# Expert weights of a mixture-of-experts block held in separated pieces of 2 KB and 1 KB

## Chip, cores and metric

The kernel runs on one core of one Trainium2 chip. The metric is the device time of one execution in microseconds; lower is better. The core's engines are TensorE (PE in the profile, with PEld for its weight loads), VectorE (DVE), ScalarE (ACT), GpSimd (POOL) and SyncE (SP); transfers run on 16 DMA engines, which SP and GpSimd feed from a queue each.

## The reference

One block of a perceiver-like network on 64 sequences of 32 tokens with 256 features (2048 tokens), float32 throughout. Three residual steps follow one another: cross-attention with 16 heads to a context of 257 rows for each sequence, self-attention with 4 heads within a sequence, and a mixture of 8 experts of which each token uses 2. The last one is what the change concerns:

```python
x = x + xattn(layernorm(x), ctx_512, ...)
x = x + attn(layernorm(x), ...)
x = x + ffn(layernorm(x), ...)

# ffn
scores = x @ Wr.T + br
w = softmax(scores); idx = top_k(scores + biases_N, 2)
val = w[idx] / sum(w[idx])
h = x @ Wl1[n] + bl1[n]                 # [M, 2*512] for each expert n
a, b = h[..., :512], h[..., 512:]
y[n] = (silu(a) * b) @ Wl2[n] + bl2[n]  # [M, 256]
out = sum over the token's two experts of val * y[n]
```

## The kernel before

**Tokens and experts.** The 2048 tokens are taken as 16 tiles of 128. The attention steps of neighbouring tiles are interleaved in an order written out by hand (`steps`, `last_steps`). For each tile `route` finds every token's two experts and scatters the normalized rows, with gates and token number, into `routed` in DRAM (L611, an indirect DMA on GpSimd's queue), sorted by expert. The experts then work on blocks of 128 routed rows that belong to one expert. Six "early" blocks are begun while the last two tiles are still in attention; the others are "late" blocks, 28 of which run in this execution.

**A block's steps.** `gathered` (L720, or in quarters L725 and L731) fetches the block's rows from `routed`. `prepared` transposes them and computes gates and target rows (L762 to L768). `first_half` and `second_half` each run 16 matmul instructions at L783 against the first layer's weights; ScalarE applies silu with a bias (L801), and VectorE adds the other bias and multiplies (L806). `combined` runs the second layer (L818), adds its bias (L823), multiplies by the gate (L824), and adds the rows into the output in DRAM (L825, an adding scatter on GpSimd's queue). Each L825 waits until the one before has landed, since both may add to the same output row.

**Weights.** An expert's weights lie in DRAM as two tables, `wall1` (first layer and its biases, 128 rows of W1LEN = 2056 floats for each expert) and `wall2` (second layer and its bias, 128 rows of W2LEN = 1280 floats). They are loaded into three "lanes" of SBUF (`lanes`); a lane is a pair of tiles, which in the profile are named lane, lane, and lane2a with lane2b. `weights` (L740) issues the loads on SP's queue, and the gathers stand in the same queue. A late block's load is skipped on the chip where the lane already holds that expert. The late stage's order is a loop:

```python
for b in range(lo, hi):
    if b + 3 < hi:     blocks.gathered(b + 3)
    if b + 1 < hi:     blocks.prepared(b + 1)
    blocks.first_half(b)
    if b > lo:
        blocks.combined(b - 1)
        if b - 1 + LANES < hi: blocks.weights(b - 1 + LANES, (1,))
    ...
    blocks.second_half(b)
    if b + LANES < hi: blocks.weights(b + LANES, (0,))
```

**What sets the order.** The order on SP and on TensorE is that of the program (`manual_schedule`). On VectorE, ScalarE and GpSimd a planner puts the instructions in order, from modelled durations, except where the program pins them.

Of the kernel before, what the change touches and what calls it, by code (L numbers as in the profile page):

```python
# [12 lines left out]
ALU = mybir.AluOpType  # L13
# [3 lines left out]
P = 128  # L17
D = 256
# [11 lines left out]
NE = 8  # L30
HID = 512
CAP = TOK
RW = D + NE + 1
NBK = (2 * TOK) // P + NE - 1
W1LEN = 2 * 2 * HID + 8
W2LEN = 5 * D
EARLY = 6
LATE = NBK - EARLY
BY_GPSIMD = 12
# [12 lines left out]
def block_kernel(  # L52
# [24 lines left out]
    nc = tc.nc  # L77
# [22 lines left out]
    def load(dst, src):  # L100
        nc.sync.dma_start(out=dst, in_=src)
# [35 lines left out]
    for i in range(4):  # L137
        w = slice(4 * HD * i, 4 * HD * (i + 1))
# [64 lines left out]
    for e in range(NE):  # L203
        tag, bufs, n = (("y", 4, D), ("bxT", 2, D), ("xg", 5, RW))[(e > 3) + (e > 5)]
# [10 lines left out]
    def bank(shape):  # L215
        return view(a_bank(), shape)
# [75 lines left out]
    def cross_queries(c):  # L292
# [8 lines left out]

        qh = wk.tile([P, W1LEN], FP, tag="qh", bufs=1, name=f"qh{c}")
        qh = qh[:, : XH // 2 * 2 * P].rearrange("p (m n) -> p m n", n=2 * P)
# [377 lines left out]
    lanes = []  # L681

    def lane_of_queries(i):
        flat = qp.tile([P, 8, XH, SEQ], FP, tag="q", name=f"lane{i}")
        flat = flat.rearrange("p a h n -> p (a h n)")
        lanes.append((flat[:, :W1LEN], flat[:, W1LEN : W1LEN + W2LEN]))

    def number(meta, k, b, most):
        return nc.values_load(
            meta[0:1, k, b : b + 1],  # L690
            engines=[SP],
            min_val=0,
            max_val=most,
            skip_runtime_bounds_check_because="formed from counts that bound it",
        )

    class Blocks:
# [14 lines left out]
        def gathered(self, b):  # L712

            at = number(self.meta, 0, b, NE * CAP - P)
            rows = routed[bass.ds(at, P), :]
            xg = xp.tile([P, RW], FP, tag="xg", bufs=5, name=f"xg_{self.name}{b}")
            if b < self.quarters:
                nc.sync.dma_start(out=xg, in_=rows)  # L720
                self.xgs[b] = xg, xg[:, D:]
                return
            xw = xp.tile([P, RW - D], FP, tag="xw", bufs=5, name=f"xw_{self.name}{b}")
            for a in range(4):
                nc.sync.dma_start(  # L725
                    out=xg[a * SEQ : (a + 1) * SEQ, :D].rearrange("p (c e) -> p c e", c=4),
                    in_=rows[:, a * 2 * SEQ : (a + 1) * 2 * SEQ].rearrange(
                        "(c i) e -> i c e", i=SEQ
                    ),
                )  # L730
            nc.sync.dma_start(out=xw, in_=rows[:, D:])  # L731
            self.xgs[b] = xg, xw

        def weights(self, b, layers, sure=False):
            if b not in self.experts:
                e = number(self.meta, 1, b, NE - 1)
                self.experts[b] = e, {} if sure else {"cond": number(self.meta, 2, b, 1) > 0}
            e, cond = self.experts[b]
            for i in layers:
                nc.sync.dma_start(  # L740
                    out=lanes[self.lane(b)][i], in_=(wall1, wall2)[i][bass.ds(e * P, P), :], **cond
                )

        def prepared(self, b):

# [32 lines left out]
        def of_half(self, b, half):  # L778
            w, _ = lanes[self.lane(b)]
            for j in range(4):  # L780
                for k in range(2):
                    lo = k * 2 * HID + (half * 4 + j) * P
                    nc.tensor.matmul(  # L783
                        self.ps[b][half][:, j, :].rearrange("p (c i) -> p c i", c=4),
                        w[:, lo : lo + P],
                        self.xTs[b][:, :, k, :],
                        start=(k == 0), stop=(k == 1),
                    )

        def second_half(self, b):  # L790
            self.ps[b].append(bank([4, P]))
            self.of_half(b, 1)
            w, _ = lanes[self.lane(b)]
            pa, pb = self.ps.pop(b)
            held.remove(self.banks.pop(b))
            del self.xTs[b]
            bias = 4 * HID
            sag = ptp.tile([P, 2, 4 * P], FP, tag="pt", name=f"sag_{self.name}{b}")
            sa, g = sag[:, 0, :], sag[:, 1, :]
            for j in range(4):  # L800
                nc.scalar.activation(  # L801
                    sa[:, j * P : (j + 1) * P], pa[:, j, :], AF.Silu,
                    bias=w[:, bias + j : bias + j + 1],
                )
            for j in range(4):
                nc.vector.scalar_tensor_tensor(  # L806
                    g[:, j * P : (j + 1) * P], pb[:, j, :],
                    w[:, bias + 4 + j : bias + 5 + j], sa[:, j * P : (j + 1) * P],
                    ALU.add, ALU.mult,
                )  # L810
            self.gs[b] = g

        def combined(self, b):
            _, w = lanes[self.lane(b)]
            g = self.gs.pop(b)
            py = bank([D])
            for j in range(4):
                nc.tensor.matmul(  # L818
                    py, g[:, j * P : (j + 1) * P], w[:, j * D : (j + 1) * D],
                    start=(j == 0), stop=(j == 3),  # L820
                )
            y = xp.tile([P, D], FP, tag="y", bufs=4, name=f"y_{self.name}{b}")
            nc.vector.tensor_tensor(y, py, w[:, 4 * D :], ALU.add)  # L823
            nc.vector.tensor_scalar(y, y, self.gate[:, b : b + 1], None, ALU.mult)  # L824
            nc.gpsimd.indirect_dma_start(  # L825
                out=out[:, :],
                out_offset=bass.IndirectOffsetOnAxis(ap=self.to[:, b : b + 1], axis=0),
                in_=y,
                in_offset=None,
                compute_op=ALU.add,  # L830
            )
# [345 lines left out]
    lane2 = lane2.rearrange("p h b n -> p (h b n)")  # L1177
    lane2a = wk.tile([P, W1LEN], FP, tag="qh", bufs=1, name="lane2a")
    lanes.append((lane2a, lane2[:, :W2LEN]))
    load(lanes[2][0], wall1[:P, :])  # L1180
    load(lanes[2][1], wall2[:P, :])
    blocks.weights(1, (0, 1), sure=True)

    def do(units):
# [135 lines left out]
```

## Time and profile before

| | before |
|---|---|
| median of 3 runs | 760.9 us (758.61 to 762.37) |
| profiled execution | 760.11 us, span 758.3 us |
| TensorE busy | 723.4 us (95%) |
| VectorE / ScalarE / GpSimd busy | 508.3 (67%) / 393.6 (52%) / 322.4 us (43%) |
| chain that ended last, by engine | PE 74%, DVE 9%, POOL 5%, ACT 4%, DMA 3% |
| DMA | 62335 packets, 90.85 MB, mean 120 GB/s |
| SP's queue (q1) / GpSimd's queue (q0) | 55696 packets, 80.32 MB / 6528 packets, 9.06 MB |
| loads of wall1 / wall2 written in the program | 34 / 34, of 1028 and 640 KB; the skipped ones among them move nothing |

How to read it: the profile is of one execution. A "span" is the time from its first to its last recorded instruction; the execution's own time is 1.8 us more. Busy TensorE time includes the ends of pipelined matmuls. The chain of work that ended last is followed back from the last instruction, at each step to what released it. The attention steps fill the span up to about 525 us; attention and early blocks overlap from 525 to 590 us; from 590 us on there are only late blocks.

### The profile page before, as it was taken

To read this page: it belongs to the slowest core of one execution; us is meant where nothing else is said; L and a number is where in the kernel's file an instruction comes from. 1 tells how busy PE (TensorE), PEld (TensorE's weight loads), DVE (VectorE), ACT (ScalarE), POOL (GpSimd) and SP (SyncE) were. 2 spreads that over 40 slices of the span, in tenths; PEclk is the share of its full clock that TensorE was granted. 3 is DMA by queue.
4 is the path that set the end of the run, shared out by engine and by line. 5 is a ranking of instruction groups with operands and counts; after the bars stand their busy time and mean duration, and the time that the engine had idled before them with its cause. 6 is when DMAs were issued, how large, how long until landed. Compare 5 with 4: busy or idle time off the path is not lost.

```text
span 758.3 us, 22405 instructions
## 1 busy us (share of the span) xinstructions
PE 723.4 (95%) x8402; PEld 613.9 (81%) x8402; DVE 508.3 (67%) x1968; ACT 393.6 (52%) x1168; POOL 322.4 (43%) x598
## 2 busy tenths in 40 slices
PE   8799999999999999999999999999799999999990
PEld 7688888787788878878887888887688999999990
DVE  4758868877886887788688777887467434444440
ACT  3676766765666676666567566675332221212210
POOL 2101173764748376474836647411144123322331
PEclk9999999999999999999999999999999999999996
DMA  8983332432334343233434323354513984485322
GB/s 263 248 211 88 90 87 90 137 112 74 92 96 110 87 136 99 75 93 95 113 89 123 93 75 93 98 150 144 226 22 65 354 275 57 54 252 114 53 37 22
DMA packets 62335, 90.85 MB, mean 120 GB/s; under 512 B 24144, under 2 KB 49104, under 8 KB 60688
## 3 DMA queue, kind: packets, MB, share of 16 engines
q1 hardware_dynamic: 55696, 80.32, 36.7%
q0 software_dynamic: 6528, 9.06, 6.6%
q8 instruction: 68, 1.11, 0.6%
q14 instruction: 43, 0.35, 0.1%
HBM read 113.76 MB, written 13.16 MB: 167 GB/s over the span
## 4 chain that ended last, share of the span: by engine, by line
PE 74%; DVE 9%; POOL 5%; ACT 4%; DMA 3%; issue 2%; SPq 0%; POOLq 0%; DVEq 0%
PE psum L783 14%; PE psum L390 12%; PE psum L359 12%; PE psum L334 7%; PE psum L432 7%; PE psum L818 6%; PE psum L313 3%; PE psum L414 3%; PE psum L448 3%; DMA out_x<-y_late,to_late 2%; POOL rprod L544 2%; PE psum L522 2%; POOL rprod L539 2%; PE psum L238 2%; ACT pr L371 2%
## 5 line engine op out<-in xcount | busy, mean ns | idle before, releaser
L364 ACT ACTIVATE pr<-psum,nmx 128x257 f32<-128x257 f32 x256 | 120.3, 474 | 87.1 <-DVE nmx L363 85.5
L359 PE MATMUL psum<-kvT,q 128*128 128x257 f32 x512 | 141.3, 395 | 1.5 <-ACT q L324 0.8
L390 PEld LDWEIGHTS psum<-prT,kvA 32*128 32x128 f32 x4096 | 119.6, 187 | 12.5 <-issue 5.4
L390 PE MATMUL psum<-prT,kvA 32*128 32x128 f32 x4096 | 127.2, 274 | 0.8 <-ACT pr L364 0.4
L363 DVE TENSOR_REDUCE nmx<-psum 128x1 f32<-128x257 f32 x256 | 104.5, 414 | 30.8 <-PE psum L359 29.5
L371 ACT ACTIVATE pr<-pr,inv 128x256 f32<-128x256 f32 x256 | 114.8, 502 | 14.6 <-DVE inv L369 13.6
L359 PEld LDWEIGHTS psum<-kvT,q 128*128 128x128 f32 x512 | 88.8, 190 | 25.2 <-issue 7.5
L373 DVE STREAM_TRANSPOSE prT<-pr 128x512 f32<-128x512 f32 x128 | 89.9, 703 | 20.8 <-ACT pr L371 19.6
L825 POOL DMA_INDIRECT out_x<-y_late,to_late x28 | 43.5, 1553 | 107.0 <-DMA out_x<-y_late,to_late 35.3
L544 POOL TENSOR_TENSOR rprod<-rprod 128x128 f32<-128x128 f32 x192 | 75.3, 392 | 14.3
L539 POOL TENSOR_TENSOR rprod<-xr,wr_row 128x256 f32<-128x256 f32 x96 | 70.2, 731 | 7.5 <-DVE xr L231 0.8
L398 ACT COPY cT<-psum 128x512 f32<-128x512 f32 x64 | 34.2, 586 | 70.5 <-PE psum L390 67.4
L783 PE MATMUL psum<-bxT_late,lane 128*128 128x128 f32 x576 | 69.0, 275 | 0.0
L783 PEld LDWEIGHTS psum<-bxT_late,lane 128*128 128x128 f32 x576 | 68.1, 192 | 0.9
L432 PE MATMUL psum<-xwo_sb,ov 128*128 128x256 f32 x256 | 60.2, 382 | 1.2 <-DVE ov L424 0.9
L334 PE MATMUL psum<-xqT,xwq_sb 128*128 128x256 f32 x256 | 60.7, 381 | 0.5 <-ACT xqT L239 0.5
L432 PEld LDWEIGHTS psum<-xwo_sb,ov 128*128 128x128 f32 x256 | 48.0, 190 | 10.0 <-DVE ov L424 3.6
L334 PEld LDWEIGHTS psum<-xqT,xwq_sb 128*128 128x128 f32 x256 | 48.3, 190 | 8.0 <-ACT xqT L239 0.8
L801 ACT ACTIVATE sag_late<-psum,lane 128x128 f32<-128x128 f32 x72 | 20.5, 368 | 63.7 <-PE psum L783 51.2
L364 ACT ACTIVATION_READ_ACCUMULATOR pr<-psum,nmx 128x1 f32 x256 | 51.0, 199 | 0.0
L611 POOL DMA_INDIRECT routed<-xr,rslots x32 | 33.5, 1047 | 39.6 <-DMA routed<-xr,rslots 13.7
L406 POOL TENSOR_TENSOR xb<-x,xbo_bc 128x256 f32<-128x256 f32 x16 | 11.6, 728 | 83.6 <-DVE x L438 62.2
(268 smaller groups left out, 1197.6 us busy)
## 6 DMA issues: line engine op xcount, KB each, us to landing
kvA<-in_ctx_a SPq DMA_DIRECT2D x256, 128.0 KB
lane<-in_wall SPq DMA_DIRECT2D x24, 1028.0 KB
lane<-in_wall SPq DMA_DIRECT2D x24, 640.0 KB
lane2a<-in_wall SPq DMA_DIRECT2D x10, 1028.0 KB
kvT<-in_ctx_t SPq DMA_DIRECT2D x64, 128.5 KB
lane2b<-in_wall SPq DMA_DIRECT2D x10, 640.0 KB
xg_late<-routed SPq DMA_DIRECT2D x80, 32.0 KB
x<-in_x SPq DMA_DIRECT2D x16, 128.0 KB
```

What stands on the lines that cost most here:

```text
L334: nc.tensor.matmul(pq[:, mm, :], xwq_sb[:, k, m * P : (m + 1) * P], xqT[:, k, :], start=(k == 0), stop=(k == 1),)
L359: nc.tensor.matmul(s, qb[:, g * P : (g + 1) * P], kvT, start=True, stop=True)
L363: nc.vector.tensor_reduce(nmx, s, AX.X, ALU.max, negate=True)
L364: nc.scalar.activation(pr[:, g, :], s, AF.Exp, bias=nmx, accum_out=sums[:, g : g + 1])
L371: nc.scalar.mul(pr[:, i, :ML], pr[:, i, :ML], inv[:, i : i + 1])
L373: nc.vector.transpose(prT[:, :, two, :], pr[:, two, :ML].rearrange("p g (c m) -> p c g m", c=MC))
L390: nc.tensor.matmul(psum[:, at + h, i * P : (i + 1) * P], values[n][r, c, :], prT[r, c, :, :].rearrange("p g n -> p (g n)"), start=(c == 0) ...
L432: nc.tensor.matmul(po, ov[:, m, :], xwo_sb[:, m, :], start=False, stop=(m == XH // 2 - 1))
L539: nc.gpsimd.tensor_tensor(prod, xr[:, 0:D], wr_rows[i], ALU.mult)
L544: nc.gpsimd.tensor_tensor(dst, prod[:, :n], prod[:, n : 2 * n], ALU.add)
L783: nc.tensor.matmul(self.ps[b][half][:, j, :].rearrange("p (c i) -> p c i", c=4), w[:, lo : lo + P], self.xTs[b][:, :, k, :], start=(k == 0 ...
L818: nc.tensor.matmul(py, g[:, j * P : (j + 1) * P], w[:, j * D : (j + 1) * D], start=(j == 0), stop=(j == 3),)
```

## The change

The two tables are cut into pieces, `wall1` into four of 514 floats (512 of weights and 2 of the 8 biases) and `wall2` into five of 256 floats (four of weights, one of bias). In DRAM the pieces of a row follow each other without a gap, so the tables are as large as before; only the biases' places in `wall1` move. In SBUF two unused floats (`APART`) stand behind each piece, so that W1LEN becomes 2064 floats and W2LEN 1290. The loads go through a new function, `load_layer`, whose two sides are written as (row, piece, element): a row is then 2056 or 1024 contiguous bytes in SBUF, in place of 8224 or 5120. The readers in `of_half`, `second_half` and `combined` compute their columns accordingly. Which loads there are, when each is issued, on which queue, and the order of the program's steps are as they were.

```diff
-W1LEN = 2 * 2 * HID + 8
-W2LEN = 5 * D
+PIECE1, PIECE2 = HID + 2, D
+APART = 2
+W1LEN = 4 * (PIECE1 + APART)
+W2LEN = 5 * (PIECE2 + APART)
...
+    def load_layer(i, lane, rows, **cond):
+        n = (PIECE1, PIECE2)[i]
+        nc.sync.dma_start(
+            out=lanes[lane][i].rearrange("p (a b) -> p a b", b=n + APART)[:, :, :n],
+            in_=(wall1, wall2)[i][rows, :].rearrange("p (a b) -> p a b", b=n),
+            **cond,
+        )
...
             for i in layers:
-                nc.sync.dma_start(
-                    out=lanes[self.lane(b)][i], in_=(wall1, wall2)[i][bass.ds(e * P, P), :], **cond
-                )
+                load_layer(i, self.lane(b), bass.ds(e * P, P), **cond)
...
-                    lo = k * 2 * HID + (half * 4 + j) * P
+                    a, c = divmod(8 * k + 4 * half + j, 4)
+                    lo = a * (PIECE1 + APART) + c * P
...
-            bias = 4 * HID
+
+            def bias(i):
+                at = i // 2 * (PIECE1 + APART) + HID + i % 2
+                return w[:, at : at + 1]
...
-                    bias=w[:, bias + j : bias + j + 1],
+                    bias=bias(j),
...
-                    w[:, bias + 4 + j : bias + 5 + j], sa[:, j * P : (j + 1) * P],
+                    bias(4 + j), sa[:, j * P : (j + 1) * P],
...
-            _, w = lanes[self.lane(b)]
+            layer = lanes[self.lane(b)][1].rearrange("p (a b) -> p a b", b=PIECE2 + APART)
+            layer = layer[:, :, :PIECE2]
...
-                    py, g[:, j * P : (j + 1) * P], w[:, j * D : (j + 1) * D],
+                    py, g[:, j * P : (j + 1) * P], layer[:, j, :],
...
-            nc.vector.tensor_tensor(y, py, w[:, 4 * D :], ALU.add)
+            nc.vector.tensor_tensor(y, py, layer[:, 4, :], ALU.add)
...
-    load(lanes[2][0], wall1[:P, :])
-    load(lanes[2][1], wall2[:P, :])
+    for i in range(2):
+        load_layer(i, 2, slice(0, P))
...
-        "wall1": np.concatenate([wl1, by_row("bl1", 8)], axis=1),
+        "wall1": np.concatenate(
+            [wl1.reshape(NE * P, 4, HID), by_row("bl1", 8).reshape(NE * P, 4, 2)], axis=2
+        ).reshape(NE * P, 4 * PIECE1),
```

## The prediction

> **What bounds the kernel now.** The profiled execution took 760.11 us (span 758.3 us), 0.8 us under the median of the runs, 760.9 us. TensorE is busy 95% of the span, so I first ask where the end is not TensorE's. The chain of waits, taken from 733 us on, answers it:
>
> ```profile
> 733.91 3.77 DMA out_x<-y_late,to_late
> ...
> 738.43 5.43 DMA out_x<-y_late,to_late
> ...
> 744.61 3.83 DMA out_x<-y_late,to_late
> ```
>
> The last three links are adding scatters (L825): each adds one finished block of 128 rows into the output and waits until the one before has landed. The last block's `y` is final at 741.89 (L824 starts 741.54, takes 0.35), yet its scatter starts at 749.19. A scatter that finds the queue free starts 0.3 us after its `y` (555.53 after 555.24), so 742.2 was possible: the end stands 7.0 us behind TensorE. GpSimd's timeline shows where this backlog arose (start, duration, line, operation, idle time before it with its releaser):
>
> ```profile
> 659.74 1.55 POOL L825 DMA_INDIRECT out_x<-y_late,to_late  x1 [3.20 <-DVE sag_late L806]
> 664.58 1.55 POOL L825 DMA_INDIRECT out_x<-y_late,to_late  x1 [3.29 <-DMA out_x<-y_late,to_late]
> 672.32 1.55 POOL L825 DMA_INDIRECT out_x<-y_late,to_late  x1 [6.18 <-DMA out_x<-y_late,to_late]
> 680.80 1.55 POOL L825 DMA_INDIRECT out_x<-y_late,to_late  x1 [6.94 <-DVE sag_late L806]
> 687.70 1.55 POOL L825 DMA_INDIRECT out_x<-y_late,to_late  x1 [5.35 <-DVE gate_late L764]
> 692.20 1.55 POOL L825 DMA_INDIRECT out_x<-y_late,to_late  x1 [2.95 <-DVE sag_late L806]
> ```
>
> Undisturbed, scatter follows scatter after 4.55 us; TensorE needs 5.3 us a block, so this queue could keep up. But the periods from 664.58 are 7.74, 8.48 and 6.90 us, and from 589.96 they are 8.81, 8.77, 7.86 and 6.85 us. Those are the two stretches in which experts' weights are loaded (588 to 620 and 665 to 688 us). The seven periods exceed 4.55 us by 23.6 us in all. By DMA issues with time to landing, a scatter takes a median of 7.0 us from 660 to 692 us and 3.8 us from 692 to 740 us, where no weights move.
>
> Inside such a stretch, the DMA view of 669.2 to 669.6 us shows what the packets do (q1 carries the weights, q0 the scatter):
>
> ```profile
> DMA packets 32, 0.15 MB, mean 370 GB/s; under 512 B 0, under 2 KB 16, under 8 KB 16
> ...
> q1 hardware_dynamic: 16, 0.13, 81.2%
> q0 software_dynamic: 16, 0.02, 25.2%
> ```
>
> On 16 engines that is one scatter row of 1 KB, then one weight row of 8 KB, in turn, 0.4 us a round. That a packet is a row follows from the page: 62335 less 60688 leaves 1647 packets of 8 KB or more, which are 12 executed loads x 128 rows = 1536, and 68 + 43 instruction packets. A slow scatter also starts late: that of 672.32 has no q0 packet until 676.6, 4.3 us after its issue, where the one of 749.19 has its first after 1.9 us. So the excess of about 3.4 us a scatter is some 2 us of late start and 1.6 us of alternation.
>
> **The change, part by part.** A weight row of 8224 bytes becomes four of 2056, one of 5120 becomes five of 1024. Matmul, bias, and addition counts stay as they are.
>
> *Alternation.* A scatter has 128 rows, 8 on each of 16 engines. At 25 GB/s an engine (397 GB/s over 16), an 8224-byte row is 0.33 us and a 5120-byte row 0.20 us; eight are 2.6 and 1.6 us, against 1.6 us seen (the scatter has the queue to itself in part of the time). Rows of 2056 and 1024 bytes give 0.66 and 0.33 us. I take 0.5 us.
>
> *Late start.* No row says whether it lasts for so many rows or so many bytes. If rows, it falls to a quarter (0.5 us); if bytes, 2 us remain. A plain scatter beside kvA's rows of 4 KB started as in quiet (162.16, first q0 packet by 164.0), nearer the first case, though that queue was short. I take 1.0 us and keep 0.5 to 2.0.
>
> A slowed scatter then costs 1.5 us (1.0 to 2.5) over 4.55, in place of 3.4. Its period, 6.05 us, is near TensorE's 5.5 us in the first stretch, so block 11's backlog (now 6.0 us: `y` ready 658.3, scatter 664.58) falls to about 1 us. The second stretch adds 3 x 0.75, and the blocks up to the end give back 5.3 us, as they do now (from 12.3 us at block 15, scatter 692.20 for a `y` of 679.6, to 7.0). So the backlog is gone at the end, and the last scatter waits for its own `y`: minus 6.4 us, from the 7.0 with 0.6 kept for a straggler like that of 738.43 (5.43 us). With 2.5 us the periods are 7.05: the first stretch saves 4.1 us, the second 2.0, and 0.9 us stays: minus 6.1. What is late next is TensorE's own end.
>
> The Trainium skill, "DMA: Bandwidth & Descriptors", section "Queues, rings and completion order", states that an engine drains a whole packet of some 9 to 17 descriptors from one queue before it turns to the next. That speaks against the change: eight 8 KB rows or sixteen 2 KB rows a turn would shorten the turn by half only, and the gain would still be most of the backlog. The alternation of 16 and 16 packets is against that rule for the rows in flight; the late start may be it.
>
> *Slower weights.* 1 KB rows already run at full load: in the DMA view of 13.5 to 14.0 us, while xwo_sb comes in,
>
> ```profile
> DMA packets 182, 0.19 MB, mean 373 GB/s; under 512 B 0, under 2 KB 182, under 8 KB 182
> ```
>
> against 397 GB/s in the stretch 600 to 604 us with 8 and 5 KB rows. One block's 1.708 MB take 4.30 us now, 4.55 us at 375 GB/s. Oddly long rows (kvT, 1028 bytes, 8.0 to 9.5 us: 356 to 373 GB/s) give at worst 4.80. The bounds are 0 to +0.5 us a load. In the first stretch six loads follow one another, 1.5 us at my value. The last, lane2a issued at 612.00, is there by about 618 (its 1.05 MB are the last but 0.7 of the 11.5 MB moved from 588 to 620), and the matmul that reads it starts at 621.95: 4 us of slack cover 1.5, and 3.0 too. The second load, needed at 599.81 and there at about 597.7, loses some 0.5 of its 2.1 us. In the second stretch lane2a of 677.57 is needed at 685.55 and there by 683. The cover fails below about 340 GB/s. The same skill page, section "Why small descriptors are slow (HBM only)", gives 3 cycles of 32 bytes a packet; by it the loads would take 5% longer, 4.5 us.
>
> *The gathers at 524 to 534 us* queue behind the first lane's 1.7 MB, and VectorE waits for them (1.13 and 1.22 us idle, up to 533.60), which holds TensorE by 0.93 us. Slower weights cost +0.2 us here (0 to +0.5).
>
> *The plain scatters of routed rows (L611) at 535.71 and 542.11* lie under the next weights. They start 6.4 us apart where a quiet pair is 3.0 apart (123.62, 126.65). SP's sixth gather waits for the second, and VectorE for the gather:
>
> ```profile
> 547.26 0.17 DVE L762 TENSOR_TENSOR gates_early<-xg_early,mine_early 128x8 f32<-128x8 f32 x1 [5.38 <-DMA xg_early<-routed]
> ```
>
> TensorE then idles 1.69 us before L238 (548.92). Of the 3.4 us lost here I give back 1.0 to TensorE (0 to 1.7), by the shorter late start.
>
> *Answered in one way.* An issue on SP took 0.38 us for xwo_sb's 1024 rows and 0.39 for lane2a's 128, so issue stays; where SP blocks on a full ring, the gathers queued behind it go through the same queue after the weights anyway: 0. Weight and bias reads start at other columns: the ACT passes over `pr`, whose rows are 1028 bytes apart, differ little (452 to 524 ns at L364), so 0; bound: 8 ns on each of L818's 8 matmuls a block, L752's 281 less L238's 273, 34 blocks: +2.2 us. VectorE's y addition reads 256 columns as before: 0.
>
> Sum against the profiled execution: -6.4 + 0.2 - 1.0 = -7.2 us, 760.1 to 752.9 us; from the median, **753.7 us**. All bounds on the good side (7.0 + 1.7) give 752.2; single runs stand 1.5 to 2.3 us from their median, so the range begins 1.7 us lower, at 750.5.
>
> **The rivals.** *The waits stay* (13%): the late start and the turns go by bytes or time. For it: the late starts are near 2 us behind 8 KB and mixed rows alike. Against: the 16 and 16. The stretches last 5% longer, so 0.35 more scatters are slow at 3.4 us each, and +0.2: 762.3 us. The same holds if rows were joined again to 8 KB on the way.
>
> *Small rows starve TensorE* (9%): unlike xwo_sb's, these rows begin 8 or 16 bytes off and leave gaps. At 275 GB/s the 29 us of the first stretch grow by 12.9, 4 of slack go: +8.9; the second stretch +2.8, the first lane +1.9, less the 7.2 gained: 767 us. TensorE begins to wait for lane under 340 GB/s, and below some 300 (+5.4, +1.1 and +1.4 in the same three places) the loss outweighs the gain. Against: kvA's 32-partition rows are the only ones near 240 GB/s.
>
> *Another order* (8%): the order on VectorE, ScalarE and GpSimd is planned from modelled durations; if these count rows, steps between 524 and 600 us move. The gates of six blocks placed at 531 us show that such a place costs 1 to 3 us: 751 to 757 or 761 to 766.
>
> **How the numbers follow.** The forecast case has 70%, at 750.5 to 757. Half a per cent is 3.8 us, about what can be told from no change. Faster (under 757.1): 70 + 4 = 74%. Same: 11 of the waits-stay case and 2 of the order case: 13%. Slower (over 764.7): 9 of the starved case and 2 of each of the others: 13%. The range is 750.5 to 763.0: it takes in the waits-stay case and leaves out the starved one and half of the order case.
>
> **What would show it.** Right: about 10,750 more DMA packets, only some 111 of 8 KB or more; L825's periods in both weight stretches at 5.3 to 6.5 us; the last L825 within 1 us of the last L824; the end of the chain TensorE and one scatter, not three; no wait of TensorE on lane. Wrong: periods of 7 us and over, a last scatter still 5 us behind its `y`, weight stretches under 340 GB/s, or PE waiting for lane after 590 us.

## The result and the profile after

The changed kernel takes 761.9 us (median of 20 runs, 758.28 to 766.46), the kernel before, run beside it, 761.0 us (20 runs, 758.03 to 764.71): ratio 1.0009, 95% interval 0.9988 to 1.0029. No difference can be told. In the profile the last adding scatter stands closer to its `y` than before; but the scatters beside the weight loads are little faster, and TensorE arrives later. The profiled execution of the changed kernel (758.28 us) is the lowest of its 20; a second profile follows among the experiments.

Below, L825 of before is L842, L783 is L795, L806 is L822, L818 is L835. The packets are as counted beforehand (page, queues): 10,752 more, and 73087 less 72976, so 111, of 8 KB or more.

```profile
DMA packets 73087, 90.85 MB, mean 120 GB/s; under 512 B 24144, under 2 KB 56784, under 8 KB 72976
```

The end of the chain of waits has one scatter in the place of three:

```profile
739.42 1.74 PE psum L835 x8
...
741.65 0.36 DVE y_late L841
742.01 0.67 issue
742.68 3.94 DMA out_x<-y_late,to_late
```

That scatter, the last but one, starts 0.67 us after its `y`, and the last, at 747.37, 1.1 us after its own (7.3 before). Still, TensorE is not what these two waited for. A scatter that finds its queue free starts 0.3 us after its `y` (here 557.98 after 557.69); one that stands behind another starts 0.75 us after the other has landed. The scatter ahead of these two was issued at 738.20 and landed 3.73 us later, at 741.93, which is 0.75 us before 742.68. The chain turns to TensorE there only because the `y` became ready 0.08 us after that landing. The last scatter likewise starts 0.75 us after the landing of the one at 742.68.

GpSimd's timeline in the second weight stretch still shows slow periods:

```profile
666.53 1.55 POOL L842 DMA_INDIRECT out_x<-y_late,to_late  x1 [2.98 <-DVE y_late L841]
671.15 1.55 POOL L842 DMA_INDIRECT out_x<-y_late,to_late  x1 [3.07 <-DVE y_late L840]
677.21 1.55 POOL L842 DMA_INDIRECT out_x<-y_late,to_late  x1 [4.51 <-DVE y_late L841]
683.92 1.55 POOL L842 DMA_INDIRECT out_x<-y_late,to_late  x1 [5.17 <-DVE sag_late L822]
691.49 1.55 POOL L842 DMA_INDIRECT out_x<-y_late,to_late  x1 [6.02 <-DVE gate_late L775]
```

From 671.15 on they are 6.06, 6.71 and 7.57 us, in the first stretch 7.27, 8.20, 7.82 and 7.74. The seven exceed 4.55 us by 19.5 us in all, against 23.6 before: 2.8 a scatter in place of 3.4, where 1.5 was forecast.

So the distance closed for another reason too: the `y`s come later. Of the 6.2 us by which it closed, 2.3 are later `y`s, as the next figures show. TensorE's waits from 590 to 760 us were, before,

```profile
PE psum L818 <- DVE sag_late L806: 0.5, 1, 0.5
```

and after (engine and line, releaser: us, times, longest):

```profile
PE psum L795 <- DVE sag_late L822: 1.4, 1, 1.4
PE psum L763 <- DMA xg_late<-routed: 1.1, 1, 1.1
PE psum L835 <- DVE sag_late L822: 0.5, 1, 0.5
```

To compare executions I count from the start of the last group of context matmuls (L390 before, L395 after; 527.00 and 529.05 us), since what lies ahead varies by 5.6 us between executions of the kernel before. From there to the last `y` I call TensorE's path: 214.89 us before, 217.22 after. The same 24 us of the first weight stretch, 65 to 89 us from that point, move (DMA view of before, 592.00 to 616.00)

```profile
DMA packets 2391, 9.18 MB, mean 382 GB/s; under 512 B 259, under 2 KB 1155, under 8 KB 1781
```

and (after, 594.05 to 618.05)

```profile
DMA packets 6345, 8.53 MB, mean 355 GB/s; under 512 B 259, under 2 KB 4173, under 8 KB 6342
```

So 7% less is moved in the same time (5% in the second pair of profiles, 376 and 357 GB/s). The place where it lengthens TensorE's path most is in TensorE's timeline of the second stretch (start, duration, ..., idle time before and its releaser). Before:

```profile
683.60 1.95 PE L783 MATMUL psum<-bxT_late,lane 128*128 128x128 f32 x16
685.38 1.95 PE L783 MATMUL psum<-bxT_late,lane2a 128*128 128x128 f32 x16
```

After:

```profile
686.40 1.95 PE L795 MATMUL psum<-bxT_late,lane 128*128 128x128 f32 x16
689.70 2.02 PE L795 MATMUL psum<-bxT_late,lane2a 128*128 128x128 f32 x16 [1.35 <-DVE sag_late L822]
```

The group at 689.70 reads lane2a, whose load SP issued at 681.20. VectorE's L822 is named as releaser because it ended just before, at 689.56. The group doesn't need it: in w1halves below, the same group starts at 689.71 while VectorE's step still runs until 690.05, and there the gap carries the load's name:

```profile
689.71 2.02 PE L800 MATMUL psum<-bxT_late,lane2a 128*128 128x128 f32 x16 [0.88 <-DMA lane2a<-in_wall]
```

### The profile page after: what moved, and what is told of

Its sections match the earlier page's. It is cut to its first block, busy times and chain, and to the rows that moved or that the text cites. A ratio compares the mean times of both kernels' runs of the same rounds, so it can differ in the third digit from the quotient of the medians.

```text
span 756.4 us, 22405 instructions
## 1 busy us (share of the span) xinstructions
PE 723.9 (96%) x8402; PEld 613.2 (81%) x8402; DVE 508.4 (67%) x1968; ACT 393.8 (52%) x1168; POOL 322.2 (43%) x598
## 2 busy tenths in 40 slices
DMA packets 73087, 90.85 MB, mean 120 GB/s; under 512 B 24144, under 2 KB 56784, under 8 KB 72976
## 4 chain that ended last, share of the span: by engine, by line
PE 66%; POOL 9%; DVE 8%; DMA 7%; issue 3%; SPq 2%; ACT 2%; POOLq 0%
PE psum L795 14%; PE psum L364 11%; PE psum L395 10%; PE psum L835 7%; PE psum L437 6%; PE psum L339 5%; POOL rprod L549 3%; POOL rprod L544 3%; PE psum L453 3%; PE psum L318 3%; PE psum L419 3%; SPq L106 2%; PE psum L527 1%; DVE prT L378 1%; POOL rpart L549 1%
## 5 line engine op out<-in xcount | busy, mean ns | idle before, releaser
L395 PEld LDWEIGHTS psum<-prT,kvA 32*128 32x128 f32 x4096 | 119.3, 187 | 12.6 <-issue 5.6
L395 PE MATMUL psum<-prT,kvA 32*128 32x128 f32 x4096 | 126.7, 274 | 1.1 <-issue 0.4
L842 POOL DMA_INDIRECT out_x<-y_late,to_late x28 | 43.4, 1550 | 104.1 <-DMA out_x<-y_late,to_late 25.1
L795 PE MATMUL psum<-bxT_late,lane 128*128 128x128 f32 x576 | 69.0, 275 | 0.0
L795 PEld LDWEIGHTS psum<-bxT_late,lane 128*128 128x128 f32 x576 | 68.0, 192 | 1.0
L817 ACT ACTIVATE sag_late<-psum,lane 128x128 f32<-128x128 f32 x72 | 20.5, 368 | 63.7 <-PE psum L795 55.3
L616 POOL DMA_INDIRECT routed<-xr,rslots x32 | 33.5, 1046 | 41.8 <-DMA routed<-xr,rslots 20.3
L411 POOL TENSOR_TENSOR xb<-x,xbo_bc 128x256 f32<-128x256 f32 x16 | 11.6, 729 | 85.5 <-DVE x L443 62.4
```

What stands on the lines that cost most here:

```text
L395: nc.tensor.matmul(psum[:, at + h, i * P : (i + 1) * P], values[n][r, c, :], prT[r, c, :, :].rearrange("p g n -> p (g n)"), start=(c == 0) ...
L795: nc.tensor.matmul(self.ps[b][half][:, j, :].rearrange("p (c i) -> p c i", c=4), w[:, lo : lo + P], self.xTs[b][:, :, k, :], start=(k == 0 ...
```

## The experiments

**Which of two theories.** Theory 1: the backlog is mostly gone, and TensorE's path is longer by slower weight rows. Theory 2: the waits stayed. The first four runs repeat both kernels and take the chain of scatters out of each: every block's `y` goes by a plain scatter to a table of its own, so that none waits for another (the output then lacks the experts' part).

```diff
+            own = tc.dram_tile([TOK + P, D], FP, name=f"own_{self.name}{b}")
...
-                out=out[:, :],
+                out=own[:, :],
...
-                compute_op=ALU.add,
```

*b_again*, the kernel before once more:

> The kernel before once more, for a second profile. Theory 1: the last scatter stands 5 to 8 us behind its y, the seven slowed periods exceed 4.55 us by 20 to 26 us in all. Theory 2: the backlog varies as much in this kernel, and is 2 to 5 us here. Time 760 to 763 us.

761.8 us, ratio 1.0006 [0.9981, 1.0030]; path +0.1 us, last scatter 7.1 us behind its `y`, the seven slow periods 22.2 us over 4.55 us each.

*a_again*, the changed kernel once more:

> The changed kernel once more, to see a second profile of it beside a second one of the kernel before, since the profiled execution of after (758.28 us) is the lowest of its 20 runs. Theory 1 (the backlog of adding scatters is gone, and TensorE's path has become later by the slower weight rows): the last scatter starts within 1 us of its y, and TensorE's end, counted from the first x128 matmul group of L395 at about 527 us, is 2 to 3 us later than in the kernel before. Theory 2 (the backlog shrinks only now and then): the last scatter stands 3 to 6 us behind its y here. Time 760 to 763 us.

762.1 us, ratio 0.9990 [0.9959, 1.0021]; path +4.2 us, last scatter 2.4 us behind, which is neither below 1 nor 3 to 6. The seven slow periods exceed 4.55 us by 22.2 us, just as in b_again. Those of the second stretch are 6.53, 9.09 and 7.03 us:

```profile
672.00 1.55 POOL L842 DMA_INDIRECT out_x<-y_late,to_late  x1 [3.14 <-DMA out_x<-y_late,to_late]
678.53 1.55 POOL L842 DMA_INDIRECT out_x<-y_late,to_late  x1 [4.98 <-DMA out_x<-y_late,to_late]
687.62 1.55 POOL L842 DMA_INDIRECT out_x<-y_late,to_late  x1 [7.55 <-DMA out_x<-y_late,to_late]
694.65 1.55 POOL L842 DMA_INDIRECT out_x<-y_late,to_late  x1 [5.48 <-DVE gate_late L775]
```

*b_nochain*, before without the chain:

> The kernel before, in which each finished block is written, not added, to a scratch table of its own, so that no scatter waits for the one before; the experts' part is missing from the output. Its time is that of TensorE's path and one scatter. Theory 1: 755 to 757 us, some 5 to 7 us under the kernel before, which is what its backlog costs. Theory 2: the backlog costs little on average: 759 to 761 us.

754.9 us, ratio 0.9908 [0.9884, 0.9933]: the backlog costs the kernel before 0.92%, 7.0 us. In this run every scatter of the late blocks starts 0.3 us after its `y`, the last one too.

*a_nochain*, after without the chain:

> The changed kernel with the same edit as b_nochain. Theory 1: 3 to 5 us above b_nochain, which is what the smaller rows cost on TensorE's path, and within 2 us of the changed kernel, which has no backlog left to lose. Theory 2: equal to b_nochain within 1 us, and as far below the changed kernel as b_nochain is below the kernel before.

757.8 us, ratio 0.9948 [0.9926, 0.9970]. Between the two kernels without a chain lie 0.40%, 3.0 us (their intervals touch, at 0.9926 to 0.9933): that is what the smaller rows cost TensorE's path. Their two profiles differ by 3.6 us, 213.74 and 217.36. Between a_again (0.9990) and this lie 0.42%, 3.2 us (4.6 us by the 1.0009 of the 20 runs): that is what the chain of scatters still adds to TensorE's path after the change, in place of 7.0. The time is 4.3 us under the median of a_again, not within 2 us as theory 1 had it. The waits of TensorE in a_nochain from 590 to 760 us show the longer path, where b_nochain has only the 0.5 us of before:

```profile
PE psum L795 <- DMA lane<-in_wall: 1.0, 1, 1.0
PE psum L835 <- DVE sag_late L822: 0.5, 1, 0.5
PE psum L795 <- issue: 0.5, 1, 0.5
PE psum L763 <- DMA xg_late<-routed: 0.3, 1, 0.3
PE psum L795 <- DMA lane2a<-in_wall: 0.3, 1, 0.3
```

Block for block, a_nochain stands behind b_nochain by 1.2 us at the first early block, 2.4 from the eighth block (first stretch) and 3.6 from the 24th (second stretch).

**What sets the end.** The 7.0 us that became 3.2 are not a gain in time, since a later `y` makes that distance shorter by itself. In the four profiles with the chain, no scatter from the sixth on waits for its `y`: each `y` is at least 0.7 us old when its scatter starts. So the last scatter's start is that of the fifth plus 29 periods, and a later `y` does not move it (all counted from the point of comparison, in us):

| | fifth scatter starts | 29 periods | of these, the seven slow ones over 4.55 each | last scatter starts | last `y` |
|---|---|---|---|---|---|
| before | 62.96 | 159.2 | 23.6 | 222.2 | 214.9 |
| b_again | 62.43 | 159.7 | 22.2 | 222.1 | 214.9 |
| after | 63.58 | 154.7 | 19.5 | 218.3 | 217.2 |
| a_again | 63.30 | 158.2 | 22.2 | 221.5 | 219.1 |

What follows the last scatter takes 9.0 to 9.1 us of the span in all four. The change thus moved the end by 3.8 us in one profile, that of its fastest execution, and by 0.6 us in the other. The times of all the executions say +0.7 and -0.8 us, neither clear of zero. What lies ahead of the point of comparison is not compared here: it takes 527.00 and 532.58 us in the two profiles of before, 529.05 and 530.49 us in those of after. Theory 1 is right about TensorE's path and wrong about the scatters, which stayed nearly as slow, as theory 2 had it; the longer path lies hidden under them. What it does is set a bound: had no scatter waited for another, the changed kernel would stand 0.52% under the kernel before, as a_nochain does, less than the 0.95% that the forecast's -7.2 us are.

**Which rows.** Four kernels cut the two tables differently: `N1` pieces of `wall1` and `N2` of `wall2`, gaps only where there is more than one piece.

```diff
-PIECE1, PIECE2 = HID + 2, D
+N1, N2 = 4, 1        # w1apart; w2apart 1, 5; w1halves 2, 1; quarter 8, 10
+PIECE1, PIECE2 = 4 * HID // N1 + 8 // N1, 5 * D // N2
```

*w1apart* (4 pieces and 1):

> Only the first layer's rows (8.2 KB) are kept in four pieces of 2 KB; the second layer's stay whole at 5 KB (4,608 more packets than the kernel before instead of 10,752). Theory 1 (smaller weight rows shorten the turns that an adding scatter waits for, and cost TensorE's path time in proportion to the rows added): TensorE's path from the last context group to the last y grows by 3.0 x 4608/10752 = 1.3 us, the last scatter starts 3 to 5 us behind its y in place of 7; time 759 to 761. Theory 2 (the cost on TensorE's path is that of the 1 KB rows alone): the path doesn't grow, time 757 to 759. Theory 3 (it is that of the pieces of the first layer, which TensorE needs first): the path grows by the whole 3 us, time 761 to 763.

*w2apart* (1 and 5):

> Only the second layer's rows (5 KB) are kept in five pieces of 1 KB; the first layer's stay whole at 8.2 KB (6,144 more packets). Theory 1: TensorE's path grows by 3.0 x 6144/10752 = 1.7 us, the last scatter starts 5 to 7 us behind its y, since the 8 KB rows still stand between its own; time 761 to 763. Theory 2 (1 KB rows alone cost): path +3 us, time 762 to 764. Theory 3 (the first layer's pieces cost): path unchanged, time 760 to 761.

*w1halves* (2 and 1):

> The first layer's rows in two pieces of 4.1 KB, the second layer's whole (1,536 more packets), so that no row is over 5 KB. Theory 1: path +0.4 us, the last scatter 5 to 6 us behind its y; time 759.5 to 761. If the gain of the scatters goes by the longest row (8 KB) and the cost by the count of rows, this is the best of the four: 757 to 759.5.

*quarter* (8 and 10):

> The first layer in eight pieces of 1 KB, the second in ten of 512 bytes (24,576 more packets than the kernel before). Theory 1 (TensorE's path pays in proportion to the rows added): path +6.9 us over the kernel before, the last scatter within 1 us of its y; time 762 to 766. Rival (the cost is that rows stand apart at all, not how many): path +3 us as with the change, backlog gone, time 757 to 759.

**Whose rows, and their bytes.** In lane2whole and lane2apart the gap depends on the lane. The "112" pair moves 112 of 128 rows, the "cut" pair seven eighths of each row, in every load but the first of each lane; their outputs aren't the reference's. The second diff is that of a_112.

```diff
-APART = 2
+APART = (2, 2, 0)    # lane2whole; lane2apart (0, 0, 2)
```

```diff
-                load_layer(i, self.lane(b), bass.ds(e * P, P), **cond)
+                most = P if (self.name, b) in (("early", 0), ("early", 1)) else 112
+                load_layer(i, self.lane(b), bass.ds(e * P, most), most, **cond)
```

*lane2whole*:

> The kernel after with the rows of the third lane (lane2a, lane2b, and with them the first load of all) whole, those of lanes 0 and 1 in pieces. If it is each load's own rows that make it late where TensorE waits for lane2a, that wait goes: path 1 us over the kernel before, last scatter 2 us behind y, time 0.2 to 0.4% under the kernel before. If it is the rate of the queue as a whole: path 1.5 to 3 us over, time within 0.2% of before.

*lane2apart*:

> The opposite: only the third lane's rows in pieces, lanes 0 and 1 whole. If each load's own rows count: TensorE waits 1 to 2 us for lane2a, path 2 to 3 us over the kernel before, last scatter 5 us behind y, time 0.1 to 0.4% over. If the rate of the queue as a whole counts: path 0.5 to 1 us over, last scatter 5 to 6 us behind, time within 0.1% of before.

*b_112*:

> The kernel before with every load of experts' weights after the first of each lane cut to 112 of 128 rows (an eighth of its bytes left out, so the output isn't the reference's): the control for the next run. TensorE's path had no wait on weights, so it doesn't change; the two weight stretches end earlier, so one slowed scatter fewer at most: the last scatter 5 to 6 us behind its y in place of 7; time 0.1 to 0.3% under the kernel before.

*a_112*:

> The same cut in the kernel after: an eighth of bytes and of rows left out, which about makes up for its lower rate (366 GB/s in place of 402 in the weight stretch). If TensorE's path is longer because the loads of the stretches land later, their share of it (1.5 to 2.5 us) goes: path at most 1 us over the kernel before, last scatter within 3 us of its y, time 0.3 to 0.6% under the kernel before, and under the control. Rival: the path is longer for what the cut doesn't touch (SP takes 0.56 in place of 0.35 us to issue a load, TensorE and VectorE read weights with gaps): path still 2 to 4 us over the kernel before, time within 0.2% of it.

*b_cut*:

> The kernel before with an eighth of every row left out of the weight loads that follow the first of each lane (7,196 and 4,480 bytes in place of 8,224 and 5,120; all 128 rows are moved; the output isn't the reference's). Control for the next run. TensorE's path had no wait on weights and stays; the stretches end 3 to 4 us earlier, so the last scatter stands 4 to 6 us behind its y in place of 7; time 0.1 to 0.4% under the kernel before.

*a_cut*:

> The same cut in the kernel after (each piece 1,796 and 896 bytes in place of 2,056 and 1,024, as many packets as in the kernel after). If the path is longer because the loads of the stretches land later, it falls to at most 1 us over the kernel before, and the gain on the scatters shows: last scatter within 2 us of its y, time 0.4 to 0.7% under the kernel before and 0.2 to 0.5% under the control. Rival (the path is longer by what the cut leaves: the count of packets, SP's issue, TensorE and VectorE reading weights with gaps): path 2 to 4 us over, time within 0.2% of the kernel before.

All in one table, the rates, paths and periods from one profile each. Rate: of all queues, 65 to 89 us from the point above; path: over the 214.89 us of before, "clock" being the part that falls to episodes of lower TensorE clock (last section); behind: last scatter after its `y`; seven: the four periods from the fifth scatter on and the three longest of the second stretch, over 4.55 us each.

| kernel | more packets | rate, GB/s | path, us | clock, us | behind, us | seven, us | ratio |
|---|---|---|---|---|---|---|---|
| before, again | 0 | 376 | +0.1 | | 7.1 | 22.2 | 1.0006 [0.9981, 1.0030] |
| after | 10,752 | 355 | +2.3 | | 1.1 | 19.5 | 1.0009 [0.9988, 1.0029] |
| after, again | 10,752 | 357 | +4.2 | | 2.4 | 22.2 | 0.9990 [0.9959, 1.0021] |
| w1halves | 1,536 | 378 | +3.0 | 1.7 | 2.2 | 20.5 | 1.0008 [0.9989, 1.0026] |
| w1apart | 4,608 | 364 | +3.2 | | 2.4 | 22.8 | 1.0022 [1.0000, 1.0044] |
| w2apart | 6,144 | 372 | +0.6 | | 0.6 | 20.5 | 1.0034 [1.0009, 1.0059] |
| quarter | 24,576 | 302 | +13.7 | 5.1 | 0.6 | 22.0 | 1.0112 [1.0091, 1.0133] |
| lane2whole | 7,168 | 371 | +2.6 | | 2.3 | 21.9 | 1.0025 [1.0002, 1.0048] |
| lane2apart | 3,584 | 370 | +1.7 | 1.7 | 2.2 | 21.1 | 1.0020 [0.9985, 1.0055] |
| b_112 | -288 | 260 | +11.6 | 1.7 | 5.9 | 33.9 | 1.0144 [1.0114, 1.0175] |
| a_112 | 9,456 | 245 | +13.4 | 1.7 | 0.6 | 30.6 | 1.0146 [1.0112, 1.0181] |
| b_cut | 0 | 346 | 0.0 | | 3.3 | 20.3 | 0.9975 [0.9948, 1.0002] |
| a_cut | 10,752 | 337 | +3.8 | 1.7 | 2.4 | 19.9 | 0.9981 [0.9954, 1.0007] |

What follows:

*The seven periods* are the main result. With rows of 8 KB, 4 KB, 2 KB, 1 KB or 512 bytes in SP's queue they exceed 4.55 us by 19.5 to 23.6 us in all (quarter has one more slow period, of 7.5 us); only loads of 112 rows, which run at 260 GB/s or less, make them longer. So the size of the weight rows moves a scatter's slowness by little, where it was to more than halve it.

*quarter* is the clearest on TensorE's path. Twice as many pieces lower the rate to 302 GB/s, and TensorE's waits after 590 us are those on loads and gathers, with hardly any backlog left (from the 29th scatter on, each but the last starts 0.3 to 0.4 us after its `y`):

```profile
PE psum L800 <- DMA lane2a<-in_wall: 3.5, 1, 3.5
PE psum L768 <- DMA xg_late<-routed: 2.0, 4, 1.1
PE psum L800 <- DMA lane<-in_wall: 0.6, 1, 0.6
```

Without the clock's part the path is 8.6 us longer, where 3.0 x 24,576/10,752 = 6.9 was expected; the time is above the range of 762 to 766 when put on the scale of that expectation (1.0112 x 761 = 769.5). The rival, a cost that doesn't grow with the number of pieces, is out. The profile is that of the slowest of five executions.

*w1apart, w2apart, w1halves* are too close to each other for their intervals, and none is faster than the kernel before. The last scatter was expected 3 to 5, 5 to 7 and 5 to 6 us behind its `y` and stands 2.4, 0.6 and 2.2 us behind; no theory had all three. The single profiles put the longer path on the first layer's pieces (w1apart +3.2, w2apart +0.6), but the times don't confirm it: w2apart's median is no lower. Its profile is that of its fastest run (754.58 us, the median is 758.2), so I leave that open.

*lane2whole, lane2apart*: with lane2a's own rows whole, TensorE still waits 0.9 us for lane2a; with only its rows in pieces it doesn't wait for it. That is as expected if the rate of the queue as a whole counts: in these two profiles a load is late by what stands ahead of it in SP's queue, not by its own rows. The path of lane2apart is 0.0 without the clock's part, but its time is no better than the others'.

*b_112, a_112* went the other way. Loads of 112 rows move at 260 GB/s, whole rows or not:

```profile
DMA packets 1673, 6.24 MB, mean 260 GB/s; under 512 B 197, under 2 KB 837, under 8 KB 1260
```

(b_112, 592.19 to 616.19.) So the loads were slower in spite of an eighth less to move, and both expectations were missed. They still show something: the kernel before, with its rows whole, also has a path some 10 us longer (11.6 less the clock's 1.7) when its loads run at 260 GB/s, and TensorE then waits for the same two things (b_112, from 545 us on):

```profile
PE psum L754 <- DMA xg_late<-routed: 6.8, 5, 1.7
...
PE psum L785 <- DMA lane2a<-in_wall: 1.6, 1, 1.6
```

A lower rate of SP's queue is thus enough to lengthen the path, without small pieces. (The time of b_112 is longer for another reason: its scatters are slower, 33.9 us in place of 22 to 24, and the last stands 5.9 us behind its `y`.) That TensorE reads weights with gaps is out as a cause: its matmuls take as long before as after (L783 and L795 275 ns each, L818 and L835 379 to 381). SP's longer issue of a load, 0.56 us in place of 0.35, isn't separated from the rate.

*b_cut, a_cut* were to show the reverse. The cut made the loads shorter by less than the eighth: at 346 in place of 382 GB/s, seven eighths take 97% of the time; at 337 in place of 355, 92%, about what whole rows take in the kernel before. In a_cut the two weight stretches add 1.2 us to the path, in place of 1.9 and 3.9 in the two profiles of the changed kernel; the rest of its 3.8 us arose before, 1.0 in the stage of the first lane and 1.7 from the clock. That speaks for the rate, but the path was to be at most 1 us over, and the times of the pair, 0.9981 and 0.9975, don't separate: the expected lead of a_cut over b_cut wasn't there.

## Why the prediction was wrong

**Right:** what bounds the kernel before. Its end stood behind TensorE by the backlog (7.0 us by b_nochain's time, 7.0 by the forecast's reading), the backlog comes from the two weight stretches, and the packets are as counted. In part right: the alternation, the turns that scatter rows and weight rows take. In the DMA view of 605.2 to 605.6 us of after,

```profile
DMA packets 90, 0.11 MB, mean 273 GB/s; under 512 B 6, under 2 KB 68, under 8 KB 90
...
q0 software_dynamic: 43, 0.04, 67.9%
q1 hardware_dynamic: 47, 0.07, 54.1%
```

43 scatter rows go beside 47 weight rows, where 16 went beside 16. Over the whole of that scatter, issued at 599.91, 367 weight rows pass beside its 128. From the start of its first q0 packet to the end of its last, a scatter in the first stretch took 3.2 us before (mean of four) and 2.1 after, in quiet 1.4; but in the second stretch it took 2.9 us before (mean of three) and 2.9 after. Over the seven, the term was to go from 1.6 to 0.5 us over quiet; measured, it went from 1.7 to 1.1. The Trainium skill, "DMA: Bandwidth & Descriptors", section "Queues, rings and completion order", has an engine drain 9 to 17 descriptors of one queue at a time; the 16 and 16 of before, on 16 engines in 0.4 us, go against it for rows of 8 KB, and the counts with small rows, which don't name an engine, don't settle it.

**Failed step: the late start, and with it "a slowed scatter then costs 1.5 us".** This is the step that decided the time. The forecast took the late start from 2.0 us to 1.0, between "if rows" and "if bytes", as a thing that scales with the rows ahead. No run shows it scaling with them. From issue to first q0 packet (on a grid of 0.2 us), the first stretch's four scatters took 4.2, 4.4, 3.4 and 3.0 us before and 4.0, 4.8, 4.2 and 5.0 after; with pieces of 1 KB and 512 bytes (quarter) 4.4, 5.0, 3.8 and 4.0; in quiet 2.0. In the second stretch the three are 4.0, 4.4, 2.0 before, 2.4, 2.8, 2.8 after, and 3.8, 4.0, 2.2 in a_again: no steady fall there either. By the packets' own times the seven start late by 1.6 us on average before and 1.7 after (quiet: 2.1 us from issue to first packet). With the alternation's 1.1, a slowed scatter costs 2.8 us after (3.2 in a_again), over the forecast's upper bound of 2.5. So the scatters went on setting the end. The row that spoke for the low value, the plain scatter beside kvA's loads, was beside a short queue, as the forecast itself noted; the plain scatter of 535.71, under weights, had its first q0 packet only 4.2 us after its issue.

**Failed step: the slack of the second stretch.** "Lane2a of 677.57 is needed at 685.55 and there by 683" put the load's landing 5.4 us after its issue. In the profile of after the load issued at 681.20 was read at 689.70, TensorE having waited: some 8.5 us. In w1halves, it was 8.0 us (681.72 to 689.71). So such a load takes about as long as the 7.8 us that the kernel before has from issue to use (677.57 to 685.38). The packets of before say so too: the last row of that load ends at 684.2, not by 683, and in after TensorE starts 0.6 us after the last row (689.1 and 689.70). There was next to no slack. It was also issued later: 152.2 us from the point of comparison in place of 150.6, of which only 0.7 us is TensorE's own lateness by then. I had worked the landing out from the bytes of that load and not from all that stands ahead of it in the queue; SP's timeline of after shows four gathers and a `lane` load issued from 676.09 to 679.55:

```profile
676.09 2.51 SPq L738 DMA_DIRECT2D xg_late<-routed  x4
678.79 0.35 SPq L744 DMA_DIRECT2D xw_late<-routed  x1
679.55 0.56 SPq L695 DMA_DIRECT2D lane<-in_wall  x1
681.20 0.57 SPq L695 DMA_DIRECT2D lane2a<-in_wall  x1
```

The same holds for the second load of the first stretch, whose 2.1 us of slack were to lose 0.5: its last row ends at 598.9 before, not at about 597.7, and a_nochain waits 1.0 us there. SP's issue of such a load, which was to stay, went from 0.35 to 0.56 us. The term 0 should have been +2.4 on TensorE's path (3.6 less 1.2 in the comparison without chains); the time doesn't show it, as the scatters end later still. The rate was about what was forecast: 7% lower, against 5.5% at the chosen 375 of 397 GB/s and the 5% that the same skill page's section "Why small descriptors are slow (HBM only)" leads to. What was wrong was the cover. For the same reason the "point" of the starving rival, 340 GB/s, was set too low: TensorE waits at 355.

**Failed step: the pair of plain scatters.** They start 6.15 us apart (538.78, 544.93) in place of 6.40, and the first one's first q0 packet comes 4.5 us after its issue, 4.2 before: the -1.0 rested on the shorter late start and went with it. TensorE's wait behind them fell from 1.69 to 1.06 us, but it is 1.1 in b_again too. The gathers' +0.2 was low: the first early block stands 0.4 us later in after and 1.2 us later in a_nochain than in its counterpart. That takes the first-lane stage from -0.8 to between +0.4 and +1.2, and this part does reach the end, since the row of scatters starts later by it.

By the forecast's own sum, tail and path together were to move the end by -7.2 us; it moved by -3.8 and -0.6 in the two profiles and by +0.7 and -0.8 in the times. "The waits stay" came nearest, in time (762.3) and in its late starts; it had neither the shorter turns of the first stretch nor the longer path, by which the last scatter stands 1.1 and 2.4 us behind its `y` in place of 7. That both kernels take the same time is no sum of a gain and an equal loss: most of the gain never came, and the loss is hidden.

## What to carry to other kernels

When transfers follow one another without a gap to the end, their own start and periods set the time; work that feeds them can be late without being seen, and a shorter distance between the two is no gain. So compare where the last transfer starts, not how far it stands behind its data. Where one term of a delay isn't tied to the quantity that the change moves, by a row that shows both sizes, its end "stays as it is" is the one to build the sum on. Smaller rows are paid for in their own queue's rate: take each load's landing from everything that is queued ahead of it, not from its own bytes, and give slack that was worked out and not seen in a trace a price for when it is gone.

## What the runs showed of the hardware

*A scatter's late start.* From GpSimd's issue to the first packet: 2.0 to 2.2 us in quiet, 3.0 to 5.0 in the first weight stretch of before, after and quarter, for weight rows of 8 KB down to 512 bytes alike. A busy queue beside it isn't enough: before, the scatter of 680.80 started in 2.0, with q1 at 96% of the engines' time from its issue to its first packet. What sets it stays open.

*Loads of 112 rows* run at 260 GB/s (b_112) where loads of 128 such rows run at 382 (before); q1's packets take 96.6% of the engines' time in the one and 91.4% in the other. Why stays open.

*The granted clock.* After some of TensorE's waits, in some executions, the clock falls for a few microseconds. In a_cut (windows: stretch, length, busy time of the engines, PEclk, DMA share, GB/s)

```profile
552.00:560.00 8.00, 7.50 (x55) 4.73 (x56) 4.80 (x17) 1.15 (x3) 1.27 (x3) 0.79 0.00 0
552.00:555.40 3.40, 3.35 (x4) 1.52 (x5) 1.70 (x7) 0.00 (x0) 0.69 (x2) 0.50 0.00 0
```

0.79 over 8 us is 1.7 us lost: the clock is at 0.50 for 3.4 us. L453's eight matmuls take 4.51 us where they take 2.85 in the profile of after, whose wait ahead of them (L243) was 1.06 us against 1.38. But the profile of before waited 1.69 us there without an episode, and b_again, the same kernel, has episodes elsewhere (0.79 at 24 to 32 us and 0.82 at 48 to 56 us of its span), so the length of one wait doesn't settle it. The Trainium skill, "TensorE: Matmul & The Clock Gate", section "Part 1: The HAM clock gate", has the clock at half rate after an idle window of about 3.4 us, and the windows run free of the program: half of 3.4 us is the 1.7 us seen, and a free-running window fits its coming and going; that it takes a whole window without work, as its table says, doesn't fit a wait of 1.4 us. Over the 20 runs of after, each thousandth of mean clock goes with 0.86 us of time (correlation -0.76). That ties much of the spread of some 8 us between runs of one kernel to the clock, without showing which of the two is the cause; a single profile's path has to be read with its clock beside it.
